# A two-layer graph network on one Trainium2 core: first stage of batch element 0 kept by nodes, biases loaded through ScalarE's queue

## The chip, the cores and the metric

The kernel runs on one core of one Trainium2 chip. The metric is the device time of one execution in microseconds (us). The time before is 2379.16 us, the median of 4 runs (2378.61 to 2379.35). All work is in float32. About 0.2% of this time is what a measurement of this kernel can tell from no change.

## The reference, cut to what matters

There are 16 batch elements, each with 1024 nodes of 128 features (`x`) and a 1024x1024 adjacency matrix `adj`. Two residual layers follow each other; only the first one's arithmetic is touched by the change, and only for batch element 0:

```python
degree = adjacency_matrix.sum(axis=-1)[:, :, None]
sum_neighbors = jnp.einsum('bid,bij->bjd', embeddings, cost_matrix) / degree   # both matrices are adj
concatenated = jnp.concatenate([embeddings, sum_neighbors], axis=-1)
out = relu(jnp.einsum('bnk,dk->bnd', concatenated, W) + b)
x1 = _layernorm(x + out)
```

The second residual layer runs four graph layers on `x1`. Each needs the adjacency scaled by its row norms for one aggregation (through a transposed copy, called `at` in the kernel) and by its column norms for the other (in place, in `a`).

## The kernel before, in words

The kernel is written engine by engine: every engine's instructions run in the order in which the Python code issues them (`manual_schedule`, line 1125). What one engine does next to another is decided by semaphores alone. A block is 128 nodes; `h` is a half of 512 nodes (four blocks); half 1 is worked before half 0.

Batch element 0 has a prologue of its own (lines 1131 to 1345), in which nothing of an earlier element can hide anything:

- `load_pair` and `load_nodes` (lines 1138 to 1156) bring the adjacency in four pairs of blocks, `PAIRS[0]` to `PAIRS[3]`, two of the four partition groups of a pair on the sync engine's queue (SP), two on GpSimd's. Behind them SP issues the weights of the four graph layers (`fetch_weights`, line 184), two sets of bias rows (`load_biases`, line 1163: nine and eight loads of 512 bytes) and the four quarters of adjacency rows, `rows[2]`, `rows[3]`, `rows[0]`, `rows[1]` (`load_rows`, line 669), from which the transposed copy `at` is made.
- As each pair lands, ScalarE squares it (`square`), VectorE sums its rows into degrees (`degree`), GpSimd adds up squares (`add_square`), and TensorE multiplies it with the nodes (`gather`, line 1237) into one PSUM bank per half, `pa[1]` and `pa[0]`.
- Then comes the first residual layer's tail: the inverse degrees are turned into a row spread over all partitions (`degree_row`, line 1257: four transposes and a ScalarE copy), VectorE multiplies `pa[h]` with it (`scaled`), TensorE applies both halves of `W` by features (`weights_of_x`, `weights_of_agT`), ScalarE does the ReLU with the bias as a column, TensorE transposes back to nodes, VectorE adds `x` (`with_x`, line 1271). `norm_stats` and `norm_factors` (lines 491 and 509) give mean and inverse deviation (VectorE `bn_stats`/`bn_aggr`, a power on GpSimd), `norm_write` (VectorE) and `norm_write_act` (ScalarE) normalize, `to_x1` (line 1280) transposes into `x1T`.
- `fold_begin` (line 200) and `fold_end` (line 224) multiply the graph layers' weights with each other. Each uses a "small" PSUM tile, of which there are two in turn (`small`, line 243), so a third such tile waits until ScalarE or VectorE has read the first.
- `row_inverses` (line 399) and `gather_inverses` (line 408) make `rinv`, the inverse row norms by which ScalarE scales the rows (`scale_rows`, line 684) before VectorE transposes them (`transpose_rows`, line 690).

After the prologue, element 0's first graph layer is `plain_layer` (line 889): a list of 34 matmul steps, with `hooks` (line 1423) that issue other engines' work before a given step. Steps 2 to 9 fill the bank `Dn[1]`, 10 to 17 `Dn[0]`, 18 to 25 `Z[1]` with `at[1]`, 26 to 33 `Z[0]` with `at[0]`. Before: `second0` (step 11) scales columns and reads `Dn[1]`; step 14 scales `rows[1]`; `first0` (step 18) gives GpSimd six column scalings, then VectorE transposes `rows[0]` and `rows[1]`, reads `Dn[0]` and scales two columns; `sums0` (step 26) makes sums of quarters (`combine_1`, `combine`), with `finish(1)` between them. `finish(0)` (line 906: an addition on VectorE, a tanh on ScalarE) stands behind everything. Then `messages` (line 727) for the second graph layer needs these tanh results: its first two groups those of half 1, its third and fourth those of half 0.

DMAs carry one of eight completion semaphores in turn. An issue waits until the last DMA on its semaphore has landed. SP's and ScalarE's DMAs take turns on the same eight; GpSimd's have their own.

Of the kernel before, what the change touches and what calls it, by code (L numbers as in the profile page):

```python
# [8 lines left out]
F32 = mybir.dt.float32  # L9
# [5 lines left out]
P = 128  # L15
# [8 lines left out]
def adj_resnorm_kernel(ctx: ExitStack, tc: tile.TileContext, x, adj, w0, b0, layers, out):  # L24
# [159 lines left out]
    def fetch_weights(raw, l, q, bc, wm=None):  # L184
        ws, bs, wd, bd, wn, bn, wu, bu = layers[l]
        nch = CHUNKS[l]
        size = max(3 * nch * P, KEPT[l] * 2 * P, WIDTH[l])
        flat = raw.take(size) if wm is None else wm[:, WIDTH[l]:]
        wr = flat[:, :3 * nch * P].rearrange("p (k c v) -> p k c v", k=3, c=nch)
        for k, w in enumerate((ws, wd, wn)):  # L190
            q.dma_start(wr[:, k], w.rearrange("(c p) v -> p c v", p=P))
        wur = raw.take(3 * P).rearrange("p (k v) -> p k v", k=3)
        q.dma_start(wur, wu.rearrange("(c p) v -> p c v", p=P))
        if wm is not None:
            wm = as_chunks(wm, l)
# [160 lines left out]
    def factor_bank(k, h, inv, name):  # L356

        pb = small(name, [HW])
        for q in range(BPH):
            i = k * NB + h * BPH + q  # L360
            nc.tensor.transpose(pb[:, q * P:(q + 1) * P], inv[:, i:i + 1].to_broadcast([P, P]), ident)
        return pb
# [800 lines left out]
    def load_biases(i, q, s=slice(None)):  # L1163
        for k, v in list(enumerate(biases_of[i]))[s]:
            q.dma_start(in_rows[k:k + 1, i * P:(i + 1) * P], v.rearrange("(o p) -> o p", o=1))

    def bias_columns(i):
        n = len(biases_of[i])
        pt = small(f"biases{i}")
        nc.tensor.transpose(pt[:, :n], in_rows[:n, i * P:(i + 1) * P], ident[:n, :n])  # L1170
        nc.scalar.copy(columns[i], pt[:, :n])
        if i == 0:
            nc.scalar.copy(b0c, pt[:, :1])
# [3 lines left out]
    def to_xT(h):  # L1177
        pt = small(f"xtr0_{h}", [HW])
        for q in range(BPH):
            nc.tensor.transpose(pt[:, q * P:(q + 1) * P], xn[:, h * BPH + q], ident)  # L1180
        nc.scalar.copy(nodes(xT[:, half(h)]), blocks(pt))

    pt = product("idle")
    for _ in range(3):
# [9 lines left out]
    places[1] = one.tile([P, 2 * NJ, HW // 2], F32, tag="T2", name="rows1_0")  # L1194
    rows, fetched = {}, []
    for l, q in enumerate((None, None, 2, 3)):
        if l in (1, 2):
            load_biases(l - 1, nc.sync)
        fetched.append(fetch_weights(raw, l, nc.sync, bcs[l], None if l else wm))
        if q is not None:  # L1200
            rows[q] = load_rows(0, q, [places[q]])
    wm = as_chunks(wm, 0)
# [21 lines left out]
    def square(i):  # L1224
        nc.scalar.activation(sq[i], a[:, i, :], AF.Square, accum_out=cols[:, i:i + 1])

    def add_square(i):
        nc.gpsimd.tensor_add(sq[4], sq[4], sq[i])
# [4 lines left out]
    def degree_inverses(h):  # L1233
        s = slice(2 * NB + h * BPH, 2 * NB + (h + 1) * BPH)
        nc.vector.reciprocal(inv[:, s], cols[:, s])

    def gather(h, i):
        nc.tensor.matmul(pa[h], xn[:, i], a[:, i, half(h)], start=(i == BPH), stop=(i == BPH - 1))

    def squares_of(h, k):  # L1240
        for i in range(h * BPH + k, h * BPH + k + 2):
            square(i)
            degree(i)

    def gathers_of(h, k):
        for i in range(h * BPH + k, h * BPH + k + 2):
            for h2 in (1, 0):
                gather(h2, i)

    agT = one.tile([P, N], F32, tag="f1T", name="agT0")  # L1250
    yT = one.tile([P, N], F32, tag="f23T", name="yT0")
    x1n = two.tile([P, NB, D], F32, tag="sq", name="x1n0")
    x1T = one.tile([P, N], F32, tag="xb", name="x1_0_T")
    dinv = one.tile([P, N], F32, tag="acc", name="dinv0")
    pn, pw = {}, {}

    def degree_row(h):
        nc.scalar.copy(nodes(dinv[:, half(h)]), blocks(factor_bank(2, h, inv, f"dinv0_{h}")))

    def scaled(h):  # L1260
        nc.vector.tensor_mul(agT[:, half(h)], pa[h], dinv[:, half(h)])

    def weights_of_x(h):
        pw[h] = product(f"pw0_0_{h}")
        nc.tensor.matmul(pw[h], w0T[:, 0], xT[:, half(h)], start=True, stop=False)

    def weights_of_agT(h):
        nc.tensor.matmul(pw[h], w0T[:, 1], agT[:, half(h)], start=False, stop=True)
        nc.scalar.activation(blocks(yT[:, half(h)]), nodes(pw[h]), AF.Relu, bias=b0c)

    def with_x(h):

        pt = ps_t.tile([P, BPH, P], F32, tag="pt", name=f"yn0_{h}")
        for q in range(BPH):
            i = h * BPH + q
            nc.tensor.transpose(pt[:, q], yT[:, i * P:(i + 1) * P], ident)
        pn[h] = x1n[:, h * BPH:(h + 1) * BPH]
        nc.vector.tensor_add(pn[h], pt, xn[:, h * BPH:(h + 1) * BPH])

    def to_x1(h):  # L1280
        pt = product(f"x1tr_{h}")
# [1 line left out]
            nc.tensor.transpose(pt[:, q * P:(q + 1) * P], x1n[:, h * BPH + q], ident)  # L1283
        nc.scalar.copy(x1T[:, half(h)], pt)

    weights_of_x(1)
    squares_of(*PAIRS[0])
    gathers_of(*PAIRS[0])
    squares_of(*PAIRS[1])
    gathers_of(*PAIRS[1])  # L1290
    to_xT(0)
    nc.vector.tensor_add(sq[6], sq[6], sq[7])
    add_square(5)
    add_square(6)
    degree_inverses(1)
    degree_row(1)
    squares_of(*PAIRS[2])
    gathers_of(*PAIRS[2])
    add_square(0)
    add_square(1)  # L1300
    first, second = 2, 3
    nc.scalar.activation(sq[second], a[:, second, :], AF.Copy, accum_out=cols[:, 2 * NB + second:2 * NB + second + 1])
    degree(first)
    gather(1, first)
    gather(1, second)
    bias_columns(0)
    degree_inverses(0)
    degree_row(0)
    scaled(1)
    weights_of_agT(1)  # L1310
    gather(0, first)
    square(first)
    gather(0, second)
    add_square(first)
    scaled(0)
    with_x(1)
    weights_of_x(0)
    weights_of_agT(0)
    stats = {1: norm_stats(pn[1], range(BPH), "0_0_1", True)}
    fold_begin(0, fetched[0])  # L1320
    with_x(0)
    fold_end(0, fetched[0])
    square(second)
    other_half = norm_stats(pn[0], range(2), "0_0_0", then=True)
    for q in range(2, BPH):
        norm_write(pn[1][:, q], pn[1][:, q], stats[1], q)
    stats[0] = other_half(range(2, BPH))
    root_inverses(cols, inv, slice(NB))
    add_square(second)
    biases = fold_begin(1, fetched[1], nc.vector.tensor_copy, True)  # L1330
    for q in range(2):
        norm_write_act(pn[1][:, q], pn[1][:, q], stats[1], q)
    to_x1(1)
    biases()
    fold_end(1, fetched[1])
    for q in range(BPH):
        norm_write(pn[0][:, q], pn[0][:, q], stats[0], q)


    kept = scratch.tile([N, D], F32, tag="kept", name="kept0")  # L1340
# [2 lines left out]
        for g in range(G):  # L1343
            nc.sync.dma_start(kv[g], x1n[g * C:(g + 1) * C, h * BPH:(h + 1) * BPH])
    at = [transposed(0, h) for h in range(NH)]
    back = rinv = None

    for b in range(B):  # L1350
# [8 lines left out]
        if b == 0:  # L1359
# [4 lines left out]
            def second_x1():  # L1364
                bias_columns(1)
                fold_begin(2, fetched[2])
                ahead["spread"] = row_inverses(0, inv)
                ahead["tr"] = column_transpose(0, st0)

            def factors_and_fold():  # L1370
                nonlocal rinv
                to_x1(0)
                fold_end(2, fetched[2])
                column_reduce(0, st0, ahead["tr"])
                rinv = gather_inverses(0, ahead["spread"])

            ahead = {}
            t = messages(b, 0, feats, wm, {0: second_x1, 1: factors_and_fold, 2: row_factors0}, with_sums=False)
# [2 lines left out]
            def columns0(rows, h, engine=nc.vector):  # L1381
                scale_columns(a, cinv[0], rows, half(h), engine)
# [13 lines left out]
            def second0(destination, finish):  # L1396
                columns0(range(NJ, NB), 1)
                destination(1, cinv[0])
                columns0(range(NJ), 1)

            def fold_and_scale(l, q):
# [1 line left out]
                scale_rows(rows[q], q, rinv)  # L1403

            def first0(destination, finish):
                columns0(range(NJ, NB), 0, nc.gpsimd)
                columns0(range(2), 0, nc.gpsimd)
                for q in (0, 1):
                    transpose_rows(rows[q], q, at)
                destination(0, cinv[0])  # L1410
                columns0(range(2, NJ), 0)

            def sums0(destination, finish):
                combine_1(y)
# [5 lines left out]
            def folded(l, part):  # L1420
# [1 line left out]

            hooks = {0: weights0, 2: lambda *_: inverses(0, st0, NB), 3: rows0, 6: cinv0,
                     9: lambda *_: fold_and_scale(3, 0), 11: second0, 12: folded(3, fold_end),
                     14: lambda *_: scale_rows(rows[1], 1, rinv), 18: first0, 26: sums0}
            T = combined(0, "T")
            plain_layer(b, 0, feats, t, wm, a, at, f1, "acc", hooks)
            wm = message_weights(b, 1)
# [382 lines left out]
```

## Time and profile before

| what | us |
|---|---|
| median of 4 runs | 2379.16 |
| the profiled execution's own time | 2379.29 |
| its span in the profile | 2377.2 |
| TensorE busy | 2364.9 |
| VectorE busy | 2092.2 |
| ScalarE busy | 981.8 |
| GpSimd busy | 282.6 |

The granted TensorE clock is at full speed in all slices. All later times are counted from the start of the span. A timeline row gives start, length, engine, line, operation, output and inputs, shape, how many instructions are merged in it, and in brackets how long the engine sat idle before it and what ended that. The merged length is the last end less the first start. A row of the groups of one line gives least, median and largest length in ns. A row of the waits gives who waited for whom, the total in us, how often, and the longest.

### The profile page before, as it was taken

How to read it: one execution, taken by the hardware profiler on the slowest of the kernel's cores; microseconds unless marked ns; L12 is line 12 of the kernel's file. 1: busy time of each engine (PE TensorE's matmuls, PEld its weight loads, DVE VectorE, ACT ScalarE, POOL GpSimd, SP SyncE). 2: the span in 40 equal slices, each digit the busy share in tenths (PEclk: the TensorE clock that was granted, in tenths of full speed). 3: DMA queues.
4: the chain of work that ended last, by engine and by line, in shares of the span. 5: the costliest groups of instructions: out<-in, count | busy, mean ns of one | idle time of the engine just before them, and what ended most of it. 6: DMA issues, size and time to landing. Idle time of an engine off the chain costs nothing.

```text
span 2377.2 us, 39260 instructions
## 1 busy us (share of the span) xinstructions
PE 2364.9 (99%) x15259; PEld 1304.6 (55%) x15259; DVE 2092.2 (88%) x2821; ACT 981.8 (41%) x1859; POOL 282.6 (12%) x104
## 2 busy tenths in 40 slices
PE   8999999999999999999999999999999999999998
PEld 5455555555555555555655555555555555555555
DVE  6999998998989989889988889898899998998954
ACT  5425334352443524435243452534425334352322
POOL 5100111101111011110011110111100111101100
PEclk9999999999999999999999999999999999999999
DMA  9537253362733527245273442635426263362410
GB/s 203 130 86 148 57 137 76 79 142 49 155 65 95 119 51 168 51 104 108 61 158 67 101 95 72 149 68 117 90 71 146 58 137 76 78 143 49 100 22 22
DMA packets 363403, 232.03 MB, mean 98 GB/s; under 512 B 150369, under 2 KB 334322, under 8 KB 363218
## 3 DMA queue, kind: packets, MB, share of 16 engines
q1 hardware_dynamic: 360578, 226.18, 43.1%
q0 software_dynamic: 816, 2.49, 0.4%
q8 instruction: 121, 1.98, 0.4%
q10 hardware_dynamic: 1824, 0.85, 0.1%
q14 instruction: 64, 0.52, 0.1%
HBM read 209.59 MB, written 19.84 MB: 97 GB/s over the span
## 4 chain that ended last, share of the span: by engine, by line
PE 98%; DMA 1%; DVE 0%; SPq 0%; issue 0%; ACT 0%; POOLq 0%; POOL 0%; DVEq 0%
PE m L1094 43%; PE z L1094 26%; PE pt L249 9%; PE pt_z L249 5%; PE m_f L624 5%; PE z_f L624 2%; PE m3s L1094 2%; PE pw L249 2%; PE z L913 1%; PE d L913 1%; PE pt_p L249 1%; DMA wm<-in_L_gnn_ws_dram 1%; DMA a<-in_adj_dram 0%; PE wm L229 0%; PE wtr L207 0%; PE pv L254 0%
## 5 line engine op out<-in xcount | busy, mean ns | idle before, releaser
L1094 PE MATMUL m<-a,t 128*64 128x512 f32 x1008 | 426.6, 593 | 0.0
L1094 PE MATMUL m<-at,t 128*64 128x512 f32 x1008 | 420.4, 592 | 0.0
L1094 PE MATMUL m<-T,S 128*64 128x512 f32 (+1 forms) x1040 | 398.6, 572 | 0.0
L1094 PE MATMUL m<-Q,S 128*64 128x512 f32 x880 | 392.3, 592 | 0.0
L484 POOL TENSOR_TENSOR rs<-ve,mhalf 128x32 f32<-128x32 f32 x30 | 192.1, 6405 | 1018.8 <-DVE ve L482 1018.8
L1094 PE MATMUL z<-at,t 128*64 128x512 f32 (+1 forms) x520 | 229.6, 579 | 0.0
L1094 PE MATMUL z<-a,S 128*64 128x512 f32 x504 | 228.3, 592 | 0.0
L1094 PE MATMUL z<-Q,t 128*64 128x512 f32 (+1 forms) x520 | 227.5, 580 | 0.0
L1094 PE MATMUL z<-a,t 128*64 128x512 f32 (+1 forms) x520 | 227.4, 580 | 0.0
L1094 PE MATMUL z<-at,S 128*64 128x512 f32 x504 | 226.6, 592 | 0.0
L1094 PEld LDWEIGHTS m<-Q,S 128*64 128x64 f32 x880 | 119.4, 137 | 188.0 <-issue 187.3
L1094 PEld LDWEIGHTS m<-T,S 128*64 128x64 f32 x1040 | 132.9, 137 | 124.4 <-issue 119.3
L1094 PEld LDWEIGHTS m<-at,t 128*64 128x64 f32 x1008 | 133.4, 137 | 115.4 <-issue 115.4
L1094 PEld LDWEIGHTS m<-a,t 128*64 128x64 f32 x1008 | 131.3, 137 | 99.1 <-issue 94.1
L946 ACT COPY e<-m 64x512 f32<-64x512 f32 x63 | 36.7, 582 | 339.0 <-PE m L1094 338.6
L1094 PE MATMUL z<-T,t 128*64 128x512 f32 (+2 forms) x400 | 173.0, 575 | 0.0
L397 POOL TENSOR_TENSOR inv<-cols,mhalf 128x16 f32<-128x16 f32 (+1 forms) x16 | 50.0, 3125 | 935.3 <-DVE cols L396 935.3
L436 DVE TENSOR_TENSOR a<-a,cinv 128x512 f32<-128x512 f32 x250 | 154.6, 694 | 0.0
L324 ACT ACTIVATE sq<-a 128x1024 f32<-128x1024 f32 x120 | 125.9, 1050 | 33.0 <-DVE acc L331 19.1
L1094 PEld LDWEIGHTS z<-Q,t 128*64 128x64 f32 x520 | 69.6, 137 | 107.6 <-issue 107.3
L249 PEld LDWEIGHTS pt<-wm,f1T 128*64 128x64 f32 x1536 | 110.8, 137 | 27.2 <-issue 14.9
L319 ACT ACTIVATE a<-a 128x1024 f32<-128x1024 f32 x120 | 125.3, 1045 | 0.4
(328 smaller groups left out, 4997.1 us busy)
## 6 DMA issues: line engine op xcount, KB each, us to landing
a<-in_adj_dram SPq DMA_DIRECT2D x120, 512.0 KB
rows<-in_adj_dram SPq DMA_DIRECT2D x480, 64.0 KB
a<-in_adj_dram SPq DMA_DIRECT2D x240, 128.0 KB
wm<-wsave SPq DMA_DIRECT2D x32, 704.0 KB
wm<-wsave SPq DMA_DIRECT2D x31, 320.0 KB
xs<-in_x_dram SPq DMA_DIRECT2D x60, 128.0 KB
cinv<-dr SPq DMA_DIRECT2D x30, 256.0 KB
dinv<-dr SPq DMA_DIRECT2D x30, 256.0 KB
```

Source lines behind the costliest of these rows:

```text
L249: nc.tensor.matmul(out[s], x[:, s], y, start=start, stop=stop)
L319: nc.scalar.activation(a[:, i, :], a[:, i, :], AF.Copy, accum_out=degree)
L324: nc.scalar.activation(sq, a[:, i, :], AF.Square, accum_out=state["cols"][:, i:i + 1])
L397: nc.gpsimd.tensor_tensor(inv[:, s], cols[:, s], mhalf[:, s], ALU.pow)
L436: engine.tensor_mul(a[:, i, s], a[:, i, s], cinv[:, s])
L484: nc.gpsimd.tensor_tensor(rstd, ve, mhalf[:, :n], ALU.pow)
L624: nc.tensor.matmul(o, x_, y_, start=start, stop=stop)
L913: nc.tensor.matmul(nodes(o) if len(y.shape) == 4 else o, x_, y, start=start, stop=stop)
L946: nc.scalar.copy(e0[high], A[high])
L1094: nc.tensor.matmul(o, x, y_, start=start, stop=stop)
```

## The change

It touches only element 0's prologue and first graph layer.

- The first residual layer's tail works by nodes. `into_rows` multiplies a block of `xT`, later of `agT`, as the stationary operand with `w0T`, so that results stand with nodes on partitions. The inverse degree is then a scalar of a partition (`with_degrees`, one `scalar_tensor_tensor` for each block), the bias a row spread over partitions (`b0r`, one new load), and the ReLU and the addition of `x` are one instruction for a half (`with_x`). The degree rows and the transposes back go away.
- The norm's statistics are made by pairs of blocks (`two_stats`).
- All 17 bias loads go from SP's queue to ScalarE's: nine ahead of everything, four behind the squares of the first pair, four behind those of the second.
- `rinv` is made inside the prologue. One squares addition goes from GpSimd to VectorE.
- In `plain_layer`, the work of step 18 on rows and on GpSimd goes to step 14 (`first_rows`), ahead of four of the column scalings. GpSimd scales four columns of half 0, not six, and VectorE four, not two.

On each engine, the order of the instructions behind that is unchanged.

The diff, cut to what the prediction speaks of:

```diff
+    load_biases(0, nc.scalar, slice(0, 5))
+    load_biases(1, nc.scalar, slice(4, 8))
+    b0r = one.tile([P, N], F32, tag="acc", name="b0r")[:, :P]
...
-        if l in (1, 2):
-            load_biases(l - 1, nc.sync)
         fetched.append(fetch_weights(raw, l, nc.sync, bcs[l], None if l else wm))
+        if l == 0:
+            nc.sync.dma_start(b0r, b0.rearrange("(o p) -> o p", o=1).to_broadcast([P, P]))
...
+    def into_rows(name, xs, k, h):
+        pw[k, h] = ps_t.tile([P, BPH, P], F32, tag="pt", name=f"{name}_{h}")
         for q in range(BPH):
             i = h * BPH + q
-            nc.tensor.transpose(pt[:, q], yT[:, i * P:(i + 1) * P], ident)
+            nc.tensor.matmul(pw[k, h][:, q], xs[:, i * P:(i + 1) * P], w0T[:, k], start=True, stop=True)
+    def gathered(h):
+        nc.scalar.copy(blocks(agT[:, half(h)]), nodes(pa[h]))
+    def x_and_bias(h):
+        nc.vector.tensor_add(xw[:, rows_of(h)], pw[0, h], b0r[:, None, :].to_broadcast([P, BPH, P]))
+    def with_degrees(h, qs):
+        for q in qs:
+            i = h * BPH + q
+            nc.vector.scalar_tensor_tensor(xw[:, i], pw[1, h][:, q], inv[:, 2 * NB + i:2 * NB + i + 1], xw[:, i],
+                                           op0=ALU.mult, op1=ALU.add)
+    def with_x(h):
+        s = rows_of(h)
+        nc.vector.scalar_tensor_tensor(x1n[:, s], xw[:, s], 0.0, xn[:, s], op0=ALU.max, op1=ALU.add)
...
     squares_of(*PAIRS[0])
+    load_biases(0, nc.scalar, slice(5, 9))
     gathers_of(*PAIRS[0])
     squares_of(*PAIRS[1])
+    load_biases(1, nc.scalar, slice(0, 4))
     gathers_of(*PAIRS[1])
...
     gather(1, second)
+    square(first)
+    degree_inverses(0)
+    x_and_bias(1)
+    gathered(1)
+    into_rows("px", xT, 0, 0)
+    into_rows("pg", agT, 1, 1)
+    square(second)
+    nc.vector.tensor_add(sq[1], sq[1], sq[first])
+    add_square(1)
+    x_and_bias(0)
+    gather(0, first)
     bias_columns(0)
     gather(0, second)
+    gathered(0)
+    with_degrees(1, range(BPH))
     with_x(1)
+    root_inverses(cols, inv, slice(NB))
+    two_stats(1, 0, True)
+    biases = fold_begin(0, fetched[0], later=True)
+    into_rows("pg", agT, 1, 0)
+    two_stats(1, 2)
+    biases()
     fold_end(0, fetched[0])
     add_square(second)
+    spread = row_inverses(0, inv)
+    with_degrees(0, range(2))
+    written(1, 0, norm_write_act)
+    biases = fold_begin(1, fetched[1], later=True)
+    for q in range(1, BPH):
+        written(1, q)
+    rinv = gather_inverses(0, spread)
     to_x1(1)
     biases()
     fold_end(1, fetched[1])
+    with_degrees(0, range(2, BPH))
+    with_x(0)
+    two_stats(0, 0)
+    two_stats(0, 2)
...
+            def first_rows(destination, finish):
+                scale_rows(rows[1], 1, rinv)
+                columns0(range(NJ, NB), 0, nc.gpsimd)
+                for q in (0, 1):
+                    transpose_rows(rows[q], q, at)
                 columns0(range(NJ), 1)
...
             def first0(destination, finish):
-                columns0(range(NJ, NB), 0, nc.gpsimd)
-                columns0(range(2), 0, nc.gpsimd)
-                for q in (0, 1):
-                    transpose_rows(rows[q], q, at)
                 destination(0, cinv[0])
-                columns0(range(2, NJ), 0)
+                columns0(range(NJ), 0)
...
-                     14: lambda *_: scale_rows(rows[1], 1, rinv), 18: first0, 26: sums0}
+                     14: first_rows, 18: first0, 26: sums0}
```

More of the change, by code (lines that the diff above doesn't have):

```diff
@@ L1180, in to_xT @@
             nc.tensor.transpose(pt[:, q * P:(q + 1) * P], xn[:, h * BPH + q], ident)
-        nc.scalar.copy(nodes(xT[:, half(h)]), blocks(pt))
+        nc.scalar.copy(xT[:, half(h)], pt)
     pt = product("idle")
@@ L1250, in adj_resnorm_kernel @@
     agT = one.tile([P, N], F32, tag="f1T", name="agT0")
-    yT = one.tile([P, N], F32, tag="f23T", name="yT0")
+    xw = one.tile([P, NB, D], F32, tag="f23T", name="xw0")
     x1n = two.tile([P, NB, D], F32, tag="sq", name="x1n0")
     x1T = one.tile([P, N], F32, tag="xb", name="x1_0_T")
[L1254 to L1273, printed above, removed]
+    pw, of_half = {}, {}
+    def rows_of(h):
+        return slice(h * BPH, (h + 1) * BPH)
@@ L1274, in with_x @@
+    def into_rows(name, xs, k, h):
+        pw[k, h] = ps_t.tile([P, BPH, P], F32, tag="pt", name=f"{name}_{h}")
         for q in range(BPH):
             i = h * BPH + q
-            nc.tensor.transpose(pt[:, q], yT[:, i * P:(i + 1) * P], ident)
-        pn[h] = x1n[:, h * BPH:(h + 1) * BPH]
-        nc.vector.tensor_add(pn[h], pt, xn[:, h * BPH:(h + 1) * BPH])
+            nc.tensor.matmul(pw[k, h][:, q], xs[:, i * P:(i + 1) * P], w0T[:, k], start=True, stop=True)
+    def gathered(h):
+        nc.scalar.copy(blocks(agT[:, half(h)]), nodes(pa[h]))
@@ new lines, in two_stats @@
+    def two_stats(h, first, shifted=False):
+        if h not in of_half:
+            of_half[h] = (one.tile([P, BPH, 6], F32, tag="stats", name=f"st0_0_{h}"), [
+                two.tile([P, BPH, n] if n > 1 else [P, BPH], F32, tag=tag, name=f"{tag}0_0_{h}")
+                for tag, n in (("mv", 2), ("ve", 1), ("rst", 1), ("shift", 1))])
+        stats, (mv, ve, rstd, shift) = of_half[h]
+        s = slice(first, first + 2)
+        for q in (first, first + 1):
+            nc.vector.bn_stats(stats[:, q], x1n[:, h * BPH + q])
+            nc.vector.bn_aggr(mv[:, q], stats[:, q])
+        nc.vector.tensor_scalar_add(ve[:, s], mv[:, s, 1], LN_EPS)
+        if shifted:
+            nc.vector.tensor_scalar_mul(shift[:, s], mv[:, s, 0], -1.0)
+        nc.gpsimd.tensor_tensor(rstd[:, s], ve[:, s], mhalf[:, s], ALU.pow)
+        if shifted:
+            nc.gpsimd.tensor_mul(shift[:, s], shift[:, s], rstd[:, s])
@@ L1280, in to_x1, with written @@
+    def written(h, q, write=norm_write):
+        mv, _, rstd, shift = of_half[h][1]
+        v = x1n[:, h * BPH + q]
+        write(v, v, (mv, rstd, shift), q)
     def to_x1(h):
@@ L1284, in to_x1 @@
         nc.scalar.copy(x1T[:, half(h)], pt)
-    weights_of_x(1)
+    into_rows("px", xT, 0, 1)
     squares_of(*PAIRS[0])
+    load_biases(0, nc.scalar, slice(5, 9))
     gathers_of(*PAIRS[0])
     squares_of(*PAIRS[1])
+    load_biases(1, nc.scalar, slice(0, 4))
     gathers_of(*PAIRS[1])
@@ L1295, in adj_resnorm_kernel @@
     degree_inverses(1)
-    degree_row(1)
     squares_of(*PAIRS[2])
@@ L1299, in adj_resnorm_kernel @@
     add_square(0)
-    add_square(1)
     first, second = 2, 3
@@ L1305, in adj_resnorm_kernel @@
     gather(1, second)
-    bias_columns(0)
[L1307 to L1312, printed above, removed]
+    square(first)
[9 more added lines that the diff above has]
+    gather(0, first)
+    bias_columns(0)
     gather(0, second)
-    add_square(first)
-    scaled(0)
+    gathered(0)
+    with_degrees(1, range(BPH))
     with_x(1)
[L1317 to L1321, printed above, removed]
-    fold_end(0, fetched[0])
[L1323 to L1328, printed above, removed]
-    add_square(second)
-    biases = fold_begin(1, fetched[1], nc.vector.tensor_copy, True)
-    for q in range(2):
-        norm_write_act(pn[1][:, q], pn[1][:, q], stats[1], q)
+    root_inverses(cols, inv, slice(NB))
[4 more added lines that the diff above has]
+    biases()
+    fold_end(0, fetched[0])
+    add_square(second)
+    spread = row_inverses(0, inv)
[5 more added lines that the diff above has]
+    rinv = gather_inverses(0, spread)
     to_x1(1)
@@ L1335, in adj_resnorm_kernel @@
     fold_end(1, fetched[1])
+    with_degrees(0, range(2, BPH))
+    with_x(0)
+    two_stats(0, 0)
+    two_stats(0, 2)
     for q in range(BPH):
-        norm_write(pn[0][:, q], pn[0][:, q], stats[0], q)
+        written(0, q)
     kept = scratch.tile([N, D], F32, tag="kept", name="kept0")
@@ L1345, in adj_resnorm_kernel @@
     at = [transposed(0, h) for h in range(NH)]
-    back = rinv = None
+    back = None
     for b in range(B):
@@ L1366, in second_x1 @@
                 fold_begin(2, fetched[2])
-                ahead["spread"] = row_inverses(0, inv)
                 ahead["tr"] = column_transpose(0, st0)
             def factors_and_fold():
-                nonlocal rinv
                 to_x1(0)
@@ L1374, in factors_and_fold @@
                 column_reduce(0, st0, ahead["tr"])
-                rinv = gather_inverses(0, ahead["spread"])
             ahead = {}
```

## The prediction

> **What bounds the kernel now.** I read the busy shares first, then TensorE's own waits, then the timeline around the code that changes.
>
> ```profile
> PE 2364.9 (99%) x15259; PEld 1304.6 (55%) x15259; DVE 2092.2 (88%) x2821; ACT 981.8 (41%) x1859; POOL 282.6 (12%) x104
> ```
> ```profile
> PE pa L1238 <- DMA a<-in_adj_dram: 2.3, 2, 1.8
> PE idle L1185 <- DVE mhalf L1206: 1.5, 1, 1.5
> PE pw L1265 <- ACT w0T L1190: 0.7, 1, 0.7
> PE x1tr L1283 <- ACT x1n L529: 0.6, 1, 0.6
> PE pa L1238 <- issue: 0.5, 1, 0.5
> PE on L1728 <- DVE f23T L1723: 0.4, 1, 0.4
> PE bm L211 <- ACT wm L232: 0.3, 1, 0.3
> PE biases L1170 <- DMA biases<-in_L_gnn_bu_dram: 0.2, 1, 0.2
> ```
>
> TensorE is busy for 99% of the span, and these eight waits are all it has. All but one (`on`, at the end) lie in the first 36 us, the region that changes. So the ceiling is low: the changed code can gain only the waits after the adjacency has landed (0.6 + 0.3 + 0.2 us), some of the landing time, and the TensorE work it removes. The last part asks whether a lead would survive. It is read from the hand-over between the first and second graph layer:
>
> ```profile
> 78.84 3.78 PE L249 MATMUL pt<-wm,f1T 128*64 128x256 f32 x32
> ```
> ```profile
> 63.15 2.36 DVE L696 STREAM_TRANSPOSE at<-Q 128x1024 f32<-128x1024 f32 x2
> 65.44 2.33 DVE L696 STREAM_TRANSPOSE at<-rows 128x1024 f32<-128x1024 f32 x2
> 67.69 0.65 DVE L904 TENSOR_TENSOR e<-d,cinv 128x512 f32<-128x512 f32 x1
> 68.27 1.27 DVE L436 TENSOR_TENSOR a<-a,cinv 128x512 f32<-128x512 f32 x2
> 69.64 2.29 DVE L715 TENSOR_TENSOR a<-a 128x2048 f32<-128x2048 f32 x1
> ...
> 79.18 0.68 DVE L907 TENSOR_TENSOR e<-e,z 128x512 f32<-128x512 f32 x1
> ```
> ```profile
> 55.79 3.29 ACT L688 ACTIVATE Q<-Q,rinv 128x256 f32<-128x256 f32 x8
> ...
> 60.48 3.30 ACT L688 ACTIVATE rows<-rows,rinv 128x256 f32<-128x256 f32 x8
> ...
> 79.89 0.72 ACT L1107 ACTIVATE f1T<-e,bout 128x512 f32<-128x512 f32 x1 [4.28 <-DVE e L907]
> ```
>
> VectorE runs without a pause and reaches `finish(0)` at 79.18. The tanh ends at 80.61. The third group of `pt`, the first that needs it, starts after two groups of 0.93 us, at 78.9 + 1.86 = 80.77. VectorE's chain is thus just 0.1 us ahead: it is co-critical, though no wait shows it.
>
> **The change part by part.** Times are those of the profiled execution (2379.29; its span is 2377.2; the median of the runs is 0.13 lower).
>
> *Front.* The built program gives SP's and ScalarE's DMAs the same eight completion semaphores, so the new bias loads take turns between the adjacency loads. SP's first adjacency load now waits until the second x block has landed, and the second until the third. The landing records put these at 3.55 and 4.1 us; the loads were issued at 2.59 and 3.07. SP's stream starts 1 us late, the first pair lands at about 11.4 (10.5 before), and its gathers (3.44) end at 14.9. The second pair lands near 15.5; its gathers and `to_xT(0)` (0.44) end at 19.4. The third pair was complete at 19.74, held by GpSimd's share, which I assume to gain while SP's queue is silent. I take a start at 19.45, 0.3 sooner; the bounds are 0.35 sooner (TensorE is not free earlier) and 0.95 later (all streams shift). ScalarE's nine early issues cost 0.25 (SP's bias rows) to 0.43 us each (its own `xn` issues at 124.89). Even at 3.9 us in all, plus the table load of 1.28, they are over at 5.9, before the copy at 6.69. The other eight go into ScalarE's gaps while it waits for pairs.
>
> *TensorE's work from there.* Removed after 19.75: four `dinv` and eight `yn` transposes (0.11 each) and three `pw` products (0.86 each): 3.9 us. Added: twelve 128x128 products, priced at 2.01/9 = 0.22 by the `wm` row L229 (nine products in 2.01): 2.7. That is 1.2 less.
>
> *Path to the first `pt` (36.98 before).* From 19.45: six gathers (5.16) end at 24.6, `px` for half 0 at 25.5. `pa[1]` is readable at 24.8, ScalarE's copy (0.59) ends at 25.4, so `pg` for half 1 runs at once to 26.4. Gather, bias transpose and gather go to 28.25. ScalarE copies `pa[0]` to 29.05, hidden by `wtr`/`bm` (0.9, to 29.15). Then `pg` for half 0 to 30.05, `wm` 30.7, `wtr` 31.05; `bm` waits for two ScalarE reads as it did before and ends at 32.1. The bias wait (0.2) is gone.
>
> VectorE beside it: `with_degrees` from 26.55. This form is not in the trace; the bounds are 0.26 (`bn_stats`, 128x128) and 0.41 (L525 from PSUM), and I take 0.3, so 27.75. `with_x` reads two SBUF tensors while GpSimd adds squares (2.36, from 25.95 to 28.3). What such a meeting costs is in these two rows, the same operation without and with a GpSimd addition beside it:
>
> ```profile
> L403 DVE TENSOR_TENSOR both<-inv,group x15: 183/184/186, 121.9 to 2164.5; 128x32 f32<-128x32 f32 x15
> L403 DVE TENSOR_TENSOR sp<-inv,group x1: 1880/1880/1880, 38.7 to 38.7; 128x32 f32<-128x32 f32 x1
> ```
>
> So I let `with_x` (0.69, as L1278) begin at 28.3 and end at 29.0. It could cost nothing (27.75 to 28.45). The Trainium skill, "SBUF — State Buffer", section "SBUF: two separate sides", says that VectorE with two SBUF inputs and GpSimd take a shared port in turn, for whole instructions. It speaks against this edit: by it `with_x` waits 0.55; without it the lead below would be 0.5 larger.
>
> GpSimd then makes the row inverses (128x8: 1.63) to 30.75, a power of two columns (0.70, L518's smallest), the shift (0.20) to 31.7, a second power to 32.4. ScalarE writes block 0 to 32.2 and copies `wtr` to 32.7, which frees the small PSUM tile for `rp` (0.27, to 33.0). VectorE writes the other three blocks by 33.05. `x1tr` (0.5) ends at 33.6, ScalarE's copy of it at 34.3, and its two reads of `bm` (0.3 + 0.27) at 34.85. Only then is there a small tile for `wm`, 0.67, to 35.5. So `pt` starts 1.5 sooner; `rp` is already done (0.27 at 42.5 before). **Lead: 1.8 us**, bounds 0.5 (front late) to 2.4 (no lock). The first-layer norm of half 0 ends at about 38.9, `x1tr` for it is due at 39.0: just covered.
>
> *Rows.* SP no longer issues 17 bias loads; `Q` is issued at about 25.2, not 30.6. ScalarE's 2.5 us wait for `Q` (before L688 at 49.50) goes. It was not on TensorE's path.
>
> *`first_rows`.* ScalarE's scaling of `rows[0]` and `rows[1]` follows weight copies that TensorE's place in the list paces: ends at 59.1 and 63.8 less the lead. VectorE must now wait for both before it may scale columns: idle from 57 to 59.1 and from 61.5 to 63.8. Then transposes 2.35, four columns 2.5 (0.62 each when GpSimd is quiet; its four are over by 64), `Dn[0]` 0.6, four columns 2.5: `combine_1` starts at 71.7, not 69.64, and `finish(0)` at 81.24 less the lead. The tanh is ready 1.48 later, at 82.72; TensorE wants it at 80.77, both less the lead. **New wait: 1.95 us.** It would be 0 if VectorE's gaps filled, and 4.6 if the four columns still met GpSimd (5.13 in place of 2.46).
>
> *Sum:* 2379.29 - 1.8 + 1.95 = 2379.4; against the median, **2379.3 us**. The gain ahead is handed back at one place.
>
> **The rivals.**
> - *The lead is kept* (chance 0.20): VectorE makes up its gaps before `finish(0)`. For it: it was never idle there before, and is relieved of the contention in 58.1 to 63.2. Against: its work now hangs on ScalarE's last row. 2379.2 - 1.8 = 2377.4 (2376.8 to 2378.4).
> - *The wait is there, the lead is not* (0.20): late first pairs, or a longer chain of small PSUM tiles. 2379.2 + 1.95 - 0.5 = 2380.6, up to 2382.0 with contention.
> - *Rows do not land sooner* (0.03), since the transfers rather than the issues limit them: row scaling keeps its old times and the lead is worth nothing: 2381.2.
> - *Slower by over 0.2%* (0.04): shared semaphores. SP's last adjacency load waits for a bias load which ScalarE issues only behind the first squares (about 13.4). With 1.2 us for that landing (the bias at 24.06) and 8.9 for an adjacency load (median of GpSimd's), the block lands at 23.5; if the bias too took 8.9, at 31.2. TensorE needs it from 23.2, and pays one for one beyond: up to 8 us, 2387. It decides from a bias landing of some 6 us on.
> - An unnamed gain of over 0.2%: 0.01.
>
> **How the numbers follow.** The forecast has 0.52 (2378.4 to 2380.4). The range 2377.0 to 2381.6 takes in it and most of the next two and leaves out about 0.13. A change of 0.2% is 4.8 us, what a measurement of this kernel can tell from no change: faster 0.01, same 0.95, slower 0.04.
>
> **What would show it.** The first `pt` row at about 35.5. VectorE's row transposes ending near 64.6, with two idle times put down to ScalarE's L688. A new TensorE wait of some 2 us of `pt` on ScalarE's tanh near 79 us. If that wait is missing, the step `first_rows` is wrong; if `pt` starts at 36.5 or later, the front or the small tiles; if `pa` waits past 23 us for the adjacency, the semaphores.

## The result, and the profile after

The changed kernel takes 2383.03 us (median; 2380.50 to 2385.29), the kernel before 2379.11 in the same jobs: a ratio of 1.0017 (95% interval 1.0012 to 1.0021). It is slower by 3.9 us, and the forecast of 2379.3 with its range up to 2381.6 was wrong. The profiled execution took 2382.80 us (span 2381.0), 3.51 more than the one of before. One execution of experiment e3, in a slow state, took 6016.55 us and stands in no ratio.

TensorE's waits in the changed kernel (who waited for whom, us in all, times, longest) show where to look:

```profile
PE pa L1242 <- DMA a<-in_adj_dram: 3.7, 1, 3.7
PE pt L249 <- ACT f1T L1107: 1.9, 1, 1.9
PE x1tr L1312 <- DVE x1n L525: 1.5, 1, 1.5
```

The first was 2.3 in two pieces before; the other two are new. `pt` on the tanh is the wait that the prediction named. `x1tr` on VectorE's L525 is not in it at all.

The products with the transposed adjacency (`z<-at`) mark the end of the changed region. They start at 66.75 us; before, at 65.01. So of the 3.51 us, 1.74 were lost ahead of that point and 1.85 at the wait for the tanh behind it; that is all of it, to 0.1 us. This sum also holds in the experiments: the time of a profiled execution, less the start of `z<-at`, less a tanh wait if there is one, is 2314.2 here, 2314.3 before, and between 2313.8 and 2314.7 in the profiled execution of each of the ten experiments.

**The loss ahead**, first the sync engine's queue (waits, then one issue of its timeline):

```profile
SPq L1141 <- DMA a<-in_adj_dram: 7.2, 1, 7.2
SPq L1141 <- DMA biases<-in_L_gnn_bs_dram: 4.7, 2, 4.0
```
```profile
23.52 0.48 SPq L1203 DMA_DIRECT2D b0r<-in_L_gnn_b_dram  x1
```

SP's eight adjacency issues, over by 7 us before, now last until 19. Two of them wait for one kind of bias load on ScalarE's queue, 4.7 us in all; the longer wait, 4.0 us, ends at 18.73, for a load that ScalarE issued at 12.57, behind its first squares. The spread bias row stands behind them and is issued at 23.52. The chain that ended last leads to it by the 7.2 us wait in the first line, not by the 4.0 us one:

```profile
4.51 9.84 DMA a<-in_adj_dram
...
14.37 8.29 DMA a<-in_adj_dram
...
23.52 3.06 DMA b0r<-in_L_gnn_b_dram
```

An adjacency load issued at 4.51 lands at 14.35. Only then does SP issue its seventh one, and a weight load ahead of the bias row waits until that has landed, at 22.66. So the bias loads delay SP in two ways: it waits for some of them, and, as they take their turns on the same eight semaphores, its own loads come to wait for one another. VectorE's timeline, with GpSimd's addition that meets it:

```profile
26.68 0.69 DVE L1274 TENSOR_TENSOR xw<-px,b0r 128x512 f32<-128x512 f32 x1 [0.96 <-DMA b0r<-in_L_gnn_b_dram]
...
30.17 1.37 DVE L1284 SCALAR_TENSOR_TENSOR x1n<-xw,xn 128x512 f32<-128x512 f32 x1
34.30 0.34 DVE L525 TENSOR_SCALAR x1n<-x1n,mv,rst 128x128 f32<-128x128 f32 x1
35.03 2.61 DVE L525 TENSOR_SCALAR x1n<-x1n,mv,rst 128x128 f32<-128x128 f32 x2 [0.39 <-POOL rst L1300]
```
```profile
34.97 2.33 POOL L1232 TENSOR_TENSOR sq<-sq,sq 128x1024 f32<-128x1024 f32 x1
```

For comparison, four such writes in the kernel before, with no such addition beside them:

```profile
36.66 1.12 DVE L525 TENSOR_SCALAR x1n<-x1n,mv,rs 128x128 f32<-128x128 f32 x4 [0.60 <-POOL rs L518]
```

The reader is to see two meetings. `with_x` (L1284) takes 1.37 instead of 0.69, a meeting that the prediction had weighed by its two L403 rows. The two writes L525 should take 0.60; they take 2.61, and the first of them ends 0.1 us after GpSimd's addition. TensorE's `x1tr` waits for exactly that. The first `pt` then starts at 38.70, not at 36.98 as before and not at 35.5 as forecast.

**The loss behind**, on VectorE and then on TensorE:

```profile
65.56 2.37 DVE L696 STREAM_TRANSPOSE at<-rows 128x1024 f32<-128x1024 f32 x2 [2.33 <-ACT rows L688]
...
82.89 0.68 DVE L907 TENSOR_TENSOR e<-e,z 128x512 f32<-128x512 f32 x1
```
```profile
84.38 1.95 PE L249 MATMUL pt<-wm,f1T 128*64 128x256 f32 x16 [1.85 <-ACT f1T L1107]
```

VectorE idles 2.09 and 2.33 us for ScalarE's scaled rows, so `finish(0)` comes at 82.89 (79.18 before) and the third group of `pt` waits 1.85 us: this is as forecast (1.95).

### The profile page after: what moved, and what is told of

The parts are those of the page before. It is cut to its first block, busy times and chain, and to the rows that moved or that the text cites. A ratio compares the mean times of both kernels' runs of the same rounds, so it can differ in the third digit from the quotient of the medians.

```text
span 2381.0 us, 39278 instructions
## 1 busy us (share of the span) xinstructions
PE 2364.9 (99%) x15267; PEld 1155.1 (49%) x15267; DVE 2095.4 (88%) x2834; ACT 980.2 (41%) x1857; POOL 276.5 (12%) x103
## 4 chain that ended last, share of the span: by engine, by line
PE 97%; DVE 1%; DMA 1%; issue 0%; ACT 0%; POOL 0%; ACTq 0%; SPq 0%; POOLq 0%; DVEq 0%
PE m L1094 44%; PE z L1094 24%; PE pt L249 9%; PE pt_z L249 5%; PE m_f L624 5%; PE m3s L1094 2%; PE z_f L624 2%; PE pw L249 2%; DMA a<-in_adj_dram 1%; PE pt_p L249 1%; PE d L913 0%; DVE a L436 0%; PE wm L229 0%; ACT rows L688 0%; DMA b0r<-in_L_gnn_b_dram 0%
## 5 line engine op out<-in xcount | busy, mean ns | idle before, releaser
L249 PE MATMUL pt<-wm,f1T 128*64 128x128 f32 (+1 forms) x1536 | 120.8, 308 | 1.9 <-ACT f1T L1107 1.9
```

The lines of the kernel that those rows point to most:

```text
L249: nc.tensor.matmul(out[s], x[:, s], y, start=start, stop=stop)
```

## The experiments

The theory after the result had three parts. (1) `first_rows` costs about 1.9 us by itself. (2) Bias loads on ScalarE's queue hold SP's loads through the shared completion semaphores, and so the bias row. (3) GpSimd's last addition blocks VectorE's L525. The rivals: the late adjacency alone, or TensorE's clock, makes the delay; or any lead is lost later anyway. All medians stand beside 2379.0 to 2379.5 for the kernel before in the same job.

### Undo `first_rows` in the changed kernel (e1)

```diff
-                     14: first_rows, 18: first0, 26: sums0}
+                     14: lambda *_: scale_rows(rows[1], 1, rinv), 18: first0, 26: sums0}
```
The row work, six GpSimd columns and two VectorE columns go back to step 18.

> The changed kernel with the work of plain_layer at its old places (rows and GpSimd's six columns at step 18, VectorE's two). Theory 1 (VectorE's row transposes wait for ScalarE, and the tanh is late): TensorE's 1.9 us wait of pt for f1T goes, VectorE no longer waits 2.1 and 2.3 us for ScalarE's rows, the time falls by 1.6 to 2.0 us against the changed kernel. Rival (that wait only shows a VectorE backlog from the prologue): the wait stays over 1 us and the time falls by less than 0.8.

Measured: 2380.65 (ratio 1.0005, 0.9996 to 1.0014), 2.4 us less than the changed kernel, a little more than the 1.6 to 2.0 expected. The wait on the tanh is gone. So part (1) holds; the 0.5 us beyond 1.9 is within what this family's runs differ by (in this run the first gathers began at 11.50, not at 12.48).

### Bias loads back on SP's queue (e2)

```diff
-    load_biases(0, nc.scalar, slice(0, 5))
-    load_biases(1, nc.scalar, slice(4, 8))
...
+        if l in (1, 2):
+            load_biases(l - 1, nc.sync)
```
and the two later groups on ScalarE's queue go as well.

> The changed kernel with all 17 bias loads back on SP's queue at their old places; the bias row b0r stays behind the first weights. Theory 1 (the shared completion semaphores hold SP's adjacency and weight loads back): the first gathers start at 10.5 again, not 12.5, TensorE keeps its full clock, b0r lands before 25, pt starts at 35.5 to 37 instead of 38.7. Rows land later again, which takes part of it back: the time falls by 1 to 2.5 us. Rival (the loads are late because the x row and the weights share the DMA engines, whichever queue issues the biases): the first gathers stay later than 11.5.

Measured: 2381.50 (1.0009, 1.0001 to 1.0018), 1.5 us less. The first gathers start at 10.11, the bias row is issued at 15.75 and nobody waits for it. `with_x` ends at 29.18 instead of 31.54, and `pt` starts at 37.03 instead of 38.70. The waits on the tanh (1.8) and on L525 (1.2) remain. Part (2) holds. The full clock that was expected did not come: it falls between 34 and 36 us, which takes back some of the 1.67 us by the start of `z` (45.23, and 46.12 in the changed kernel).

### Keep TensorE busy ahead of the first pair (e3)

```diff
+    pt = product("warm")
+    for _ in range(4):
+        nc.tensor.matmul(pt, idle[:, :P], idle, start=True, stop=True)
```
This is for the rival that the clock sets the start of `pt`. In the changed kernel the granted clock falls after TensorE's 3.67 us wait for the first pair. A row of the windows gives the stretch, its length, TensorE's busy time (and number of instructions), the granted clock, the busy share of the DMA engines and GB/s:

```profile
12.00:14.00 2.00, 1.52 (x2) 0.57 1.00 223
14.00:16.00 2.00, 2.00 (x4) 0.58 1.06 281
```

> The changed kernel with four more products of the idle tile on TensorE between px and the first gathers, so that TensorE has no pause of 3.7 us before them. Theory 1 (the prologue's end is set by the landing of b0r, VectorE, GpSimd's lock and x1tr, not by TensorE's gathers): the granted clock stays full, the second half of the gathers starts at 20.4 instead of 21.4, but pt still starts within 0.4 us of 38.7 and the time moves by less than 0.4. Rival (late gathers at half clock set it): pt starts 0.7 to 1.0 us sooner and the time falls as much, more where a run has a longer slow phase, and the runs lie closer together.

Measured: 2384.18 (1.0020, 1.0011 to 1.0029). The clock is full from 8 to 38 us and the third pair's gathers start 0.74 us sooner (20.71), yet `pt` starts at 38.67, as before the edit at 38.70. So in the changed kernel the first pairs are not on the path; VectorE's wait for the bias row (1.39) and L525 (2.62) are. The median is 1.2 us above that of the changed kernel, but the two intervals overlap, so a rise is not shown. The profiled run took 1.35 us more than that of the changed kernel, and its windows show where:

```profile
36.00:38.00 2.00, 0.59 (x4) 1.00 1.23 271
38.00:40.00 2.00, 2.00 (x12) 0.66 1.22 222
40.00:42.00 2.00, 2.00 (x11) 0.50 1.20 190
```

After a stretch in which TensorE is busy 0.68 and 0.59 us out of 2 (the waits for small tiles and for L525), it gets half its clock for about 3.4 us. From the first `pt` to `z` it takes 8.89 us, and 7.42 in the profiled run of the changed kernel, whose clock stayed full here. The runs of e1 and e2 show the same fall behind the same stretch. I had not expected this second cost of a sparse stretch.

### Leave out GpSimd's last addition (e4)

```diff
     fold_end(0, fetched[0])
-    add_square(second)
     spread = row_inverses(0, inv)
```

> The changed kernel without GpSimd's last addition of squares (add_square(second)): one block's squares are left out of the column norms. Theory 1 (VectorE's write of block 2 waits for that addition: 2.4 us in place of 0.34): L525 takes 0.34 everywhere, TensorE's 1.5 us wait of x1tr goes, pt starts at 36.8 to 37.2, the time falls by 1.4 to 1.9 us. Rival (L525 waits for the power ahead of the addition, and is only drawn long): pt starts within 0.3 us of 38.7 and the time moves by less than 0.4.

Measured: 2380.08 (1.0005, 0.9996 to 1.0014), 2.95 us less, more than the 1.4 to 1.9 expected. VectorE's writes are no longer held, and TensorE no longer waits for them:

```profile
32.66 0.60 DVE L525 TENSOR_SCALAR x1n<-x1n,mv,rst 128x128 f32<-128x128 f32 x2 [0.40 <-POOL rst L1300]
```

`pt` starts at 34.49 (36.8 to 37.2 were expected), and the clock stays full. Part (3) holds. More than the 2.0 us of the meeting is gained in this run: the first gathers began at 10.95, and no sparse stretch is left for the clock to fall behind. It is the fastest of the eleven (2378.53, 1.55 below their median), so how the 2.95 us of the median divide stays open.

### Before, with only the bias loads moved (e5)

```diff
+    load_biases(0, nc.scalar, slice(0, 5))
+    load_biases(1, nc.scalar, slice(4, 8))
...
     squares_of(*PAIRS[0])
+    load_biases(0, nc.scalar, slice(5, 9))
```
and so on, as in the change; the loads on SP go.

> The kernel before, with only the 17 bias loads moved to ScalarE's queue as in the change. It has no spread bias row. Theory 1 (the new loads hold SP's adjacency loads through the shared semaphores, and that alone delays TensorE): the first gathers start at 11.0 to 12.7 us instead of 10.5, the third pair's one to 1.7 us later than 19.75, and the time is 1.0 to 1.7 us longer than before, 2380.1 to 2380.8. Theory 2 (the late first pair is harmless by itself; in the changed kernel it counts only through the late spread bias row): the third pair's gathers start within 0.4 us of 19.75 and the time is within 0.4 us of the kernel before, 2378.7 to 2379.5.

Measured: 2380.23 (1.0006, 0.9997 to 1.0015), with runs from 2378.96 to 2383.34. In the median theory 1 holds, though the interval includes no change. The profiled run is one of the long ones (2382.66):

```profile
10.00:12.00 2.00, 0.00 (x0) 0.81 1.07 213
12.00:14.00 2.00, 1.08 (x2) 0.50 1.02 272
14.00:16.00 2.00, 2.00 (x4) 0.50 1.02 332
```

TensorE waits 4.65 us for the first pair, and its 16 gather passes then take 9.67 us (7.03 at full clock). Here TensorE itself sets the pace, so this reaches the end: `pt` at 40.45, `z<-at` at 68.49. The mean granted clock of the single runs goes with their time: 1.000 for those up to 2379.7, 0.998 for those above 2382.6.

### The same, with TensorE kept busy (e10)

The edit of e3, with three products instead of four, in the kernel of e5.

> The kernel before with the bias loads on ScalarE's queue, as in the run with that part alone, and three idle products more (0.86 us each) behind the first product with W, so that TensorE's pause before the first pair falls below 2.5 us. Theory 1 (what the late front costs where TensorE sets the pace is mostly the half clock that follows a pause of over 3 us; with the part alone, runs were spread from 2379.0 to 2383.3): the granted clock stays 1.00 from 8 to 20 us, the four gathers blocks take 7.0 to 7.6 us and not 9.7, no run is above 2381.5 and the median is 2378.8 to 2380.0. Theory 2 (the cost is the late landing itself): the clock is full too, but the third pair's gathers still start 1 us or more later than 19.75, the spread stays, and the median is 2380.0 to 2381.5.

Measured: 2379.50 (1.0001, 0.9992 to 1.0010), runs from 2378.70 to 2380.84, clock full. Even with the first pair as late as 13.83, the passes took 7.11 us. The long runs are gone: none of the eleven is above 2381, where e5 had three above 2382.6. That is as theory 1 had it, by which they came from the half clock. Of the 1.15 us that the late front costs in the median, 0.5 is left, and that would belong to the landing itself (in the profiled run, a late one, `z<-at` starts at 66.85, 1.8 us later than before). The intervals of e5 and e10 both include no change, so this division is an estimate.

### Before, with only `first_rows` (e6)

```diff
-                     14: lambda *_: scale_rows(rows[1], 1, rinv), 18: first0, 26: sums0}
+                     14: first_rows, 18: first0, 26: sums0}
```

> The kernel before, with only the work on rows[0] and rows[1] and the column scalings moved from step 18 to step 14, as in the change. Theory 1 (VectorE then waits for ScalarE's scaled rows, wherever the prologue ends): TensorE waits 1.7 to 2.4 us of pt on the tanh near 79 us, and the time is 1.6 to 2.3 us longer, 2380.7 to 2381.4. Theory 2 (the wait appears only because the front of the changed kernel is late): a wait below 0.6 us and a time within 0.6 us of the kernel before, 2379.1 to 2379.7.

Measured: 2380.98 (1.0009, 1.0000 to 1.0017), 1.9 us more than before, with the same wait of 1.85 us on the tanh. Theory 1, to 0.1 us: this part loses 1.9 us here, and the wait is 1.85 us in all five profiled runs that have it (the changed kernel, e2, e3, e4, e6), whatever stands ahead of it.

### All three places mended (e7)

The work of `first_rows` and the bias loads go back as in e1 and e2, and the addition goes to VectorE, into the messages:

```diff
-    add_square(second)
     spread = row_inverses(0, inv)
...
                 fold_begin(2, fetched[2])
-                ahead["tr"] = column_transpose(0, st0)
+                nc.vector.tensor_add(sq[4], sq[4], sq[second])
```
The transposition and the sum behind it move one hook later each, the column factors' copy by one step.

> The changed kernel with three parts undone or moved: the row work back at step 18; the bias loads back on SP's queue; the last addition of squares taken from GpSimd, where it blocks VectorE's writes, to VectorE behind the first product of the messages, with the transposition and the sum behind it one hook later each. Theory 1 (these three places hold all that the change loses, and the new tail by nodes gains about 2 us): the first pt at 34.2 to 35.2 us, no TensorE wait for the tanh, and a time 1.5 to 2.5 us below the kernel before, 2376.6 to 2377.6. Theory 2 (a lead made in the prologue is not kept, since the rows land when they did before and VectorE's chain to the tanh is co-critical): the same early pt, but a wait on the tanh of 1 to 2 us, or one for the column factors, and a time of 2378.6 to 2379.3.

Measured: 2379.06 (1.0001, 0.9992 to 1.0010): no gain. `pt` starts at 34.45, 2.5 us sooner than before, and `z` at 41.80, 2.7 sooner; `z<-at` starts at 65.17, 0.16 later. Theory 2 was right, in its second form. Of the 2.8 us that are lost from `z` to `z<-at`, 2.0 go at one place, a wait of TensorE's that is new, and 0.4 at a wait of `pc` for VectorE:

```profile
53.57 1.36 PE L207 MATMUL wtr<-ident,raw 128*128 128x128 f32 x9 [2.00 <-ACT cinv L353]
```
```profile
49.75 3.30 ACT L688 ACTIVATE Q<-Q,rinv 128x256 f32<-128x256 f32 x8 [5.53 <-DMA Q<-in_adj_dram]
52.96 1.04 ACT L353 COPY cinv<-cinvp 128x512 f32<-128x512 f32 x2
```

ScalarE takes its instructions in the order of the code. It waits 5.53 us for a quarter of the rows, scales it, and only then copies the column factors out of the PSUM tile that `wtr` needs. Before, ScalarE waited for rows too (2.5 us), but TensorE came late enough not to notice.

### Biases on ScalarE's queue, later (e8)

As e7, with nine loads behind the squares of the second pair and eight behind those of the third, none ahead.

> As the kernel with the addition on VectorE, but with the bias loads on ScalarE's queue behind the squares of the second pair (nine) and of the third pair (eight), none ahead of the adjacency. Theory 1 (only bias loads issued ahead of SP's adjacency loads hold them): the first gathers at 10.1 to 10.6 us, the rows land some 2 us sooner than with the biases on SP, and the time is 2376.4 to 2377.6. Theory 2 (any use of ScalarE's queue holds SP's weights and the bias row through the semaphores): VectorE waits for the bias row by 0.5 us or more, pt starts at 35.5 or later and the time is 2377.8 to 2379.0.

Measured: 2386.42 (1.0030, 1.0019 to 1.0041). The adjacency is no longer held: the first gathers start at 10.00. But theory 2 was right, and in a worse way than expected. ScalarE's own issues now wait:

```profile
30.91 1.06 ACT L1329 ACTIVATE sq<-a 128x1024 f32<-128x1024 f32 x1 [7.15 <-DMA Q<-in_adj_dram]
```

Here bias issues that waited for their semaphores, between 25.0 and 30.8, kept all of ScalarE idle for 7.15 us. ScalarE copies `pa[1]` late, and TensorE waits 8.2 us for it.

### The second set of biases on GpSimd's queue (e9)

As e7, with this:

```diff
-        if l in (1, 2):
-            load_biases(l - 1, nc.sync)
+        if l == 1:
+            load_biases(0, nc.sync)
...
     add_square(5)
+    load_biases(1, nc.gpsimd, slice(0, 4))
...
     add_square(0)
+    load_biases(1, nc.gpsimd, slice(4, 8))
```
and the column sums one matmul step later.

> As the kernel with the addition on VectorE, but with the second set of bias loads (eight) on GpSimd's queue in two gaps between its additions, and the column-norm sums one matmul step later. Theory 1 (the lead of 2.5 us at the first pt is lost only because ScalarE waits 5.5 us for the second quarter of rows ahead of its copy of the column factors, and eight bias loads at 0.3 us each on SP stand ahead of those rows): SP issues the first rows at 29.0 to 29.8 us instead of 31.8, ScalarE's wait falls to some 3 us, TensorE's wait of 2.0 us for the copy falls below 0.5, the products with the transposed adjacency start at 62.8 to 64.0 instead of 65.2, and the time is 1.2 to 2.4 us below the kernel before, 2376.7 to 2377.9. Theory 2 (the rows are limited by their transfers, not by SP's issues): the rows land within 0.7 us of where they did, the wait for the copy stays above 1.3 us and the time is 2378.4 to 2379.3.

Measured: 2377.87 (2376.46 to 2378.81), beside 2379.47 before in the same job: ratio 0.9992 (0.9983 to 1.0001), 1.6 us less. GpSimd's loads take 0.48 to 0.53 us each in gaps that it had. SP issues the first rows at 28.73 (31.79 in e7), ScalarE's wait falls to 4.30 and TensorE's to a fifth:

```profile
52.14 1.35 PE L207 MATMUL wtr<-ident,raw 128*128 128x128 f32 x9 [0.42 <-ACT cinv L353]
...
63.74 13.90 PE L913 MATMUL z<-at,t 128*128 128x512 f32 x32
```

`z<-at` starts 1.27 us sooner than before. This is the fastest version; its interval just includes no change. So a gain from the tail by nodes is likely, but not shown, once nothing meets VectorE's writes and the rows keep up. Not tried: the addition moved and the row work put back, with the bias loads left on ScalarE's queue. The profiled run of e4 reached `z<-at` at 62.46, sooner than this one.

## Why the prediction was wrong, step by step

- *`first_rows`*: right. The wait was put at 1.95 us; it is 1.85, in the changed kernel, in e2, e3, e4 and e6, at the place and on the engines named.
- *TensorE's work from there*: right. From the third pair's start to the end of `pg` for half 0 the working has 10.6 us (19.45 to 30.05); it took 11.0 (21.45 to 32.4). `with_degrees` was priced at 0.3 and took 0.30.
- *Front*: the mechanism was right, the size was not. "The first pair lands at about 11.4": its gathers started at 12.48, the third pair's at 21.45 instead of 19.45. I let two issues wait for nodes; but further issues waited too, the seventh 7.2 us for an adjacency load of SP's own, and the last one for a bias load that ScalarE makes only behind its first squares. That is the mechanism of my slower rival (0.04). Its condition, a bias landing of some 6 us, was met (6.16), but the last block then landed by 24.22, 5.5 us after its issue and not 8.9, and there was no wait of `pa` past 23 us.
- *Path to the first `pt`*, the bias row: not in the working. I added SP's new load of the bias row and let `with_degrees` start when the products are done. VectorE's L1274 waits 0.96 us for that row, which held the squares addition behind it and, through GpSimd's, `with_x`. It ended at 31.5 instead of 29.0: 2.5 us. Of these, 1.0 is the wait for the row, and 1.5 the late last block, whose row sums VectorE starts at 24.22 and in e2 at 22.69. In e2, with both in time, `with_x` ended at 29.18. TensorE's late gathers are no part of it: in e3 they were 0.74 sooner, and `with_x` ended at 31.51.
- *Path to the first `pt`*, "VectorE writes the other three blocks by 33.05": this step failed. I followed GpSimd up to its second power and left out the addition that stands behind it in its order. I weighed such a meeting for `with_x`, which has two SBUF tensors, and not for L525, which has one. It cost 2.0 us. In before the same addition started at 38.19, after the last of these writes.
- *Path to the first `pt`*, the small tile for `wm` (1.25 us): this step was wrong too, the other way. I let `wm` wait until ScalarE had read `bm`. But `wm` started at 37.87 and ScalarE read `bm` only at 38.55; in before, too, at 36.11 and 36.52. So `wm` takes the other of the two tiles, and they do not simply go in turn. Without this term the working gives 34.25; in e7, which has neither of the two losses, `pt` started at 34.45. So 2.5 + 2.0 - 1.25 is the 3.2 us between the forecast of 35.5 and 38.70 (to 0.05): the wrong tile hid a part of the miss.
- *Lead*: -1.8 was forecast, with -0.5 to -2.4 as bounds; +1.74 came. This term alone is the miss, 3.5 us. A bound of zero lead was too narrow: the step hung on two engines' orders that I had not both written down.
- *Rows*: sooner, though not as forecast (28.02, not 25.2), and no one needed it here; in e7, with the lead, ScalarE's wait for them cost TensorE 2.0 us, so "It was not on TensorE's path" held only without a lead. The rival "the wait is there, the lead is not" (0.20, up to 2382.0) came nearest.

## What to carry to other kernels

Write out the orders of all engines that share a resource, to the end of the stretch, before a step is called done at a time: the instruction behind the last one in the working made 2.0 us of the loss. In this kernel a load that was moved to another engine's queue still took its turn on the shared completion semaphores, and a wait for them stopped whatever stood behind the issue, on both queues (7.2 us on SP's, 7.15 us on ScalarE's in e8). A lead made early in a full kernel is worth only as much as each later stage's inputs come sooner too (here the rows of the adjacency); after each gain, look which wait is next.

## What the runs showed of the hardware that I had not expected

- VectorE's `tensor_scalar` with one SBUF tensor in and out (128x128) was held for a whole GpSimd addition: 2.36 us instead of 0.30 to 0.34. Beside GpSimd's powers it was not: in before, four such writes took 1.12 us from 36.66, with a power from 36.59 to 38.22. The Trainium skill, "SBUF — State Buffer", section "SBUF: two separate sides", names VectorE operations in a 2-port mode beside those with two SBUF inputs; I had used only the second half of that sentence. The trace agrees with its "gets the pair for the whole instruction; the other fully blocks" for the additions, and not for the powers. No row here names the mode in which L525 ran.
- After TensorE's pauses of 3.67 and 4.65 us the granted clock was half for some 3.4 and 6.8 us (worked out from the windows' means of the changed kernel and of e5), and it fell in the same way in e8's pause of 8.18 us; after pauses of 1.42 to 2.29 us (before, e1, e2, e4, e9) it stayed at 1.00. The Trainium skill, "TensorE: Matmul & The Clock Gate", section "Part 1: The HAM clock gate", gives an idle window of some 3.4 us, not tied to the kernel's start, as the condition; these pauses agree.
- The clock also fell without such a pause: in e1, e2, e3 and e6 behind 4 us in which no wait was over 1.5 us but TensorE was busy for only 1.3 to 2.9 us. It did not fall in the profiled runs of before and after, with 3.1 and 1.9 us in such a stretch, nor in e5 and e10, with 2.9 us, nor around the first pair of e1, with 1.7 us from 8 to 12. If it varies from run to run, that would fit the spread of the changed kernel's times (mean clock 0.999 at 2381, 0.997 or 0.998 from 2384 on); what decides it stays open.
- A bias load of 512 bytes took 6.2 us from its issue (12.57) to its release of SP (18.73), while the DMA engines were busy throughout (share 1.00 to 1.06 in the windows from 12 to 20); I had priced it at 1.2.
